# The recurrent state's product: keys scaled for each head on ScalarE, and the copy of px shared

## The chip, the cores and the metric

The kernel runs on one core of one Trainium2 chip, in one launch. The metric is the device time in microseconds (us), the median of several executions. A core has TensorE (PE: matmuls, and the weight loads before them), VectorE (DVE), ScalarE (ACT), GpSimd (POOL) and SyncE (SP, which issues the DMAs here). Each runs its own queue of instructions in order and waits on semaphores for the others.

## The reference

A gated delta-rule attention layer with 32 value heads of width 128 and 16 key heads, followed by a layer norm, a residual, a small gated feed-forward layer, and again layer norm and residual. The input is 4 sequences of 1024 tokens, width 256, in fp32. What concerns the change is the scan over chunks of 64 tokens:

```
def step(St, inp):
    q_i, k_i, u_i, kcd_i, dec_i, g_i = inp
    attn = einsum('bhid,bhjd->bhij', q_i, k_i) * dec_i
    v_new = u_i - einsum('bhid,bhdv->bhiv', kcd_i, St)
    inter = einsum('bhid,bhdv->bhiv', q_i * exp(g_i)[..., None], St)
    out_i = inter + einsum('bhij,bhjv->bhiv', attn, v_new)
    g_last = g_i[..., -1]
    St_new = St * exp(g_last)[..., None, None] + einsum(
        'bhid,bhiv->bhdv', k_i * exp(g_last[..., None] - g_i)[..., None], v_new)
    return (St_new, out_i)
```

The new state is the old one, decayed, plus keys times new values, summed over the 64 tokens of the chunk, where each token has a decay factor of its own for each head. A key head serves two value heads.

## The kernel before

**Tiling.** The 32 heads are taken in 8 groups of 4 (`HG = 4` value heads, `MG = 2` key heads). A tile is 128 rows: a chunk of 64 tokens from each of two sequences, called the halves `ab`. A group has 32 tiles, in four super-blocks of 8. One tile of one group is a step, so there are 256 of them, and the state of two pairs of sequences alternates (`states[p]`). The last two steps of a group need no new state, so 240 steps compute one.

**One step** (`step`, a generator that is resumed in pieces):
- `pv`: values transposed on PE; ACT scales them into `x0` (L675).
- `pkqs` (L684): keys and queries times the state; DVE adds the first into `x0`, four instructions (L695); ACT scales the second into `qs` (L696).
- `px` (L704): `x0` times the inverted matrix, 4 matmuls. `px` is minus the new values, up to a factor for each token. ACT writes `xs`, a negated copy of `px` (L709). Unless the step is a last one, DVE writes `yg`, which is `px` times `ncd` (L712); PE transposes the keys into `pk` (L715), two key heads in one tile each; ACT copies them to `kt` (L717); POOL decays the state (L721).
- `po` (L704): `xs` times the attention matrix; DVE adds `qs` to make `core` (L728). ACT squares `core` (L733).
- `pu` (L741): keys times `yg`, for each key head and each half; the two value heads of a key head stand side by side in 256 columns. DVE adds `pu` to the state (L748).

`ncd` is made for four tiles at a time in `norms` (L502): minus the write strength over the squared norm of the key, times the decay to the end of the chunk.

**What surrounds it.** The program runs as a software pipeline over super-blocks. `channel` makes the convolved projections of later steps: `pp` (L423, wq or wv) on PE, a scaled copy `cv` on ACT (L437), three updates of `cv` on DVE (L440), and a last activation on ACT (L444). `invert` solves the triangular systems on DVE, one rank at a time (L580, L581). `scores` (L530 to L556) and `project_out` (`pz` L143, `zs` L782 to L786, `pto` L790, `oT` L792, `pout` L797, `ac` L802) fill in the rest. The order on every engine is the order of the program, which is written out by hand in a table with a row for each of the eight iterations of a super-block. Two of the rows:

```
SLOTS = [
    ...
    "A v1 O3 N0 v1 T J v1 O4 N1 r Z v1 B N2 q s U",
    ...
    "A v1 O3 N0 v1 T J v1 O4 v1 N1 r Z v1 B N2 q s v1 U",
```

They are rows 1 and 5, counted from 0. `N0`, `N1`, `N2` resume the newest step (`x0`, then `pkqs`, then `px` with `xs`, `yg`, `pk` and `kt`); `O3`, `J`, `O4` resume the one before (`po`, the squares, `pu`); `A` and `B` are `pp` for wv and wq; `v1` is one rank of `invert`; `T`, `Z`, `U` are pieces of `project_out`; `r`, `q`, `s` are `rms`, `roots` and `scores`. In rows 1 and 5 `q` and `s` put activations of other functions on ACT right behind `kt`, with a table load before each kind. "Place n" below means row n of this table, named by the px in it.

**Buffers.** PSUM has a pool of four single banks, taken in turn by `pv`, `pkqs`, `px`, `pk`, `po`, `pz`, `pto`, `pout` and others, and a pool of two double banks, for `pp` and `pu`. A matmul that takes a bank waits until the last reader of its previous tile is through. `xs`, `yg` and `kt` have one buffer each in SBUF.

Of the kernel before, what the change touches and what calls it, by code (L numbers as in the profile page):

```python
# [9 lines left out]
F32 = mybir.dt.float32  # L10
I32 = mybir.dt.int32
AF = mybir.ActivationFunctionType
ALU = mybir.AluOpType

P = 128
# [8 lines left out]
HG = 4  # L24
NG = NV // HG
MG = HG // 2
# [4 lines left out]
SB = 8  # L31
# [28 lines left out]
def bc(ap, shape):  # L60
    return ap.to_broadcast(shape)
# [3 lines left out]
def delta_net_ffn_kernel(  # L65
# [18 lines left out]
    V, A, G_, T_ = nc.vector, nc.scalar, nc.gpsimd, nc.tensor  # L84
# [34 lines left out]
    for ab in range(2):  # L119
        half = slice(ab * C, (ab + 1) * C)  # L120
# [73 lines left out]
    with tc.tile_pool(name="pre", bufs=2) as pre, tc.tile_pool(name="gates", bufs=1) as gp:  # L194
# [38 lines left out]
        u = gp.tile(full, F32, name="u")  # L233
# [75 lines left out]
    with ExitStack() as main:  # L309
        w1 = main.enter_context(tc.tile_pool(name="w1", bufs=1))  # L310
        w2 = main.enter_context(tc.tile_pool(name="w2", bufs=2))
# [4 lines left out]
        def t4(name, bufs=1):  # L316
            return sc.tile([P, HG, P], F32, tag=name, name=name, bufs=bufs)
# [3 lines left out]
        def as4(ps):  # L321
            return ps.rearrange("p (h i) -> p h i", h=HG)
# [128 lines left out]
        def norms(k, blk):  # L451

            if blk == 0:
                k.n2 = w2.tile([P, SB, MG, 2], F32, tag="n2", name="n2", bufs=5)
                k.cc = w2.tile([P, SB, HG], F32, tag="cc", name="cc", bufs=5)
                k.ncd = w2.tile([P, SB, HG], F32, tag="ncd", name="ncd", bufs=5)
                k.ms = w2.tile([P, SB, HG], F32, tag="ms", name="ms", bufs=5)
                k.ltd = sd.tile([P, SB, HG, C], F32, tag="ltd", name="ltd")
                k.atd = sd.tile([P, SB, HG, C], F32, tag="atd", name="atd")
                k.vd, k.vtd = (sd.tile([P, BS, BS], F32, tag=f"vd{i}", name="vd") for i in range(2))  # L460
                k.nd = sd.tile([P, NQ, BS], F32, tag="nd", name="nd")
            us = slice(4 * blk, 4 * blk + 4)

            squares = []
            for m in range(MG):
                for j in range(2):
                    src = k.qk[blk][m][:, :, :, j, :, :].rearrange("p n q a t -> p (n q) (a t)")
                    sq = sc.tile([P, 4, P], F32, tag="sq", name="sq", bufs=4)
                    A.activation(sq, src, AF.Square)
                    squares.append(sq)  # L470
                yield
            ps = bank("pn")
            for q, sq in enumerate(squares):
                T_.matmul(
                    ps[q * BS : (q + 1) * BS, :],
                    lhsT=ones,
                    rhs=sq.rearrange("p i t -> p (i t)"),
                    start=True,
                    stop=True,
                )  # L480
            nT = sc.tile([P, 4, P], F32, tag="sq", name="nT", bufs=4)
            A.copy(nT, as4(ps))
            yield
            ps = bank("pn")
            for i in range(4):
                T_.transpose(as4(ps)[:, i, :], nT[:, i, :], ident)
            n2 = k.n2[:, us]
            V.tensor_scalar_max(
                n2.rearrange("p u m j -> p u (m j)"),
                ps.rearrange("p (u q i) -> p u q i", u=4, i=BS)[:, :, :, 0],  # L490
                NRM2_MIN,
            )
            rk = w2.tile([P, 4, MG], F32, tag="rk", name="rk")
            V.reciprocal(rk, n2[:, :, :, 0])
            t0 = k.t0 + 4 * blk
            V.tensor_tensor(
                k.cc[:, us].rearrange("p u (m h) -> p u m h", h=2),
                dks[k.g][3][:, t0 : t0 + 4, :].rearrange("p u (m h) -> p u m h", h=2),
                bc(rk.unsqueeze(3), [P, 4, MG, 2]),
                ALU.mult,  # L500
            )
            V.scalar_tensor_tensor(  # L502
                k.ncd[:, us], k.cc[:, us], -1.0, dks[k.g][1][:, t0 : t0 + 4, :], ALU.mult, ALU.mult
            )

        def roots(k):
# [151 lines left out]
        def step(k, u):  # L658

            blk, un = divmod(u, 4)  # L660
            n, p = divmod(un, 2)
            ti = k.t0 + u
            ex, _, _, _, el = dks[k.g]
            first = k.first and u < 2
            last = k.last and u >= SB - 2
            S_ = states[p]
            qk, vt = k.qku.pop(u), k.vt[blk]

            pv = bank("pv")
            for h in range(HG):  # L670
                T_.transpose(as4(pv)[:, h, :], vt[h][:, un * P : (un + 1) * P], ident)
            x0 = t4("x0")
            for m in range(MG):
                two = slice(2 * m, 2 * m + 2)
                A.activation(x0[:, two, :], as4(pv)[:, two, :], AF.Copy, scale=k.nnk[:, u, m : m + 1])  # L675
            yield
            if not first:
                got = []
                for j in range(2):
                    ps = bank("pkqs")  # L680
                    for m in range(MG):
                        two = slice(2 * m, 2 * m + 2)
                        for ab in range(2):
                            T_.matmul(  # L684
                                as4(ps)[ab * C : (ab + 1) * C, two, :],
                                lhsT=qk[:, m, j, ab, :],
                                rhs=S_[:, ab, two, :],
                                start=True,
                                stop=True,
                            )  # L690
                    got.append(ps)
                qs = t4("qs")
                for h in range(HG):
                    e = ex[:, ti, h : h + 1]
                    V.scalar_tensor_tensor(x0[:, h, :], as4(got[0])[:, h, :], e, x0[:, h, :], ALU.mult, ALU.add)  # L695
                    A.activation(qs[:, h, :], as4(got[1])[:, h, :], AF.Copy, scale=e)  # L696
            yield

            ue, ae = k.exp.pop(u)

            def applied(w, src, name):
                ps = bank(name)
                for h in range(HG):
                    T_.matmul(as4(ps)[:, h, :], lhsT=w[:, h, :], rhs=src[:, h, :], start=True, stop=True)  # L704
                return ps

            px = applied(ue, x0, "px")
            xs = t4("xs")
            A.activation(xs, as4(px), AF.Copy, scale=-1.0)  # L709
            if not last:  # L710
                yg = t4("yg")
                V.tensor_tensor(yg, as4(px), bc(k.ncd[:, u, :].unsqueeze(2), h4), ALU.mult)  # L712
                pk = bank("pk")
                for m in range(MG):
                    T_.transpose(as4(pk)[:, m, :], qk[:, m, 0].rearrange("p a t -> p (a t)"), ident)  # L715
                kt = sc.tile([P, MG, P], F32, tag="kt", name="kt")
                A.copy(kt, as4(pk)[:, :MG, :])  # L717
                if not first:
                    flat = S_.rearrange("p a h d -> p (a h) d")
                    decay = el[:, ti].rearrange("p a h -> p (a h)").unsqueeze(2)  # L720
                    G_.tensor_tensor(flat, flat, bc(decay, [P, 2 * HG, P]), ALU.mult)  # L721
            yield
            po = applied(ae, xs, "po")
            core = t4("core", OUT_LAG)
            if first:
                V.tensor_copy(core, as4(po))
            else:
                V.tensor_tensor(core, as4(po), qs, ALU.add)  # L728
            k.cores[u] = core
            yield  # L730
            junk = sc.tile([P, P], F32, tag="junk", name="junk")
            for h in range(HG):
                A.activation(junk, core[:, h, :], AF.Square, accum_out=k.ms[:, u, h : h + 1])  # L733
            yield
            if not last:
                pu = two_banks("pu")
                for m in range(MG):
                    two = slice(2 * m, 2 * m + 2)
                    for ab in range(2):
                        half = slice(ab * C, (ab + 1) * C)  # L740
                        T_.matmul(  # L741
                            as4(pu[:, ab])[:, two, :], lhsT=kt[half, m, :], rhs=yg[half, two, :], start=True, stop=True
                        )
                state = S_.rearrange("p a h d -> p (a h d)")
                if first:
                    V.tensor_copy(state, pu.rearrange("p a n -> p (a n)"))
                else:
                    V.tensor_tensor(state, pu.rearrange("p a n -> p (a n)"), state, ALU.add)  # L748
# [410 lines left out]
```

## Time and profile before

| | |
|---|---|
| median of 3 runs | 4344.73 us (4342.15 to 4349.24) |
| profiled execution, its own time | 4347.06 us |
| its span in the trace | 4345.3 us, 79442 instructions |
| mean granted PE clock | 0.98 |
| PE px, 128x128 moving | 2048 records, 287 ns each, 292.9 us busy |
| PE pu, weights 64x128, 64x256 moving | 1920 records, 402 ns each, 272.2 us busy |
| DVE yg, 128x512 | 240, 683 ns each, 164.0 us |
| ACT kt, 128x256 | 240, 374 ns each, 89.6 us |
| ACT xs, 128x512 | 256, 605 ns each, 154.8 us |
| ACT qs, 128x128 with a scale for each partition | 960, 361 ns each, 269.9 us |

How to read it: every fp32 matmul of the program leaves two matmul records and two weight loads in the trace, so the 960 matmuls of `pu` are 1920 records. The records of PE overlap, so the busy time of a group is less than records times mean. In the timelines a row gives the start, the length, the engine, the line, the operation, output and input, and how many instructions were merged; in brackets the idle time before it and what ended that. Rows of the chain of waits give the start, the length, and the engine with its line. A row of the stretches gives PE, PE's weight loads, DVE, ACT and POOL, then the clock and the share of DMA.

### The profile page before, as it was taken

Reading aid. Unit: us, or ns where it says so; the run is one execution under the profiler, and the core shown is the slowest. Engines: PE = TensorE matmul, PEld = TensorE weight load, DVE = VectorE, ACT = ScalarE, POOL = GpSimd, SP = SyncE. Lnnn points to the kernel's source line nnn. Section 1 sums busy time; section 2 is a strip of 40 time slices with the busy share of each in tenths; the row PEclk is TensorE's granted clock in tenths of the full one; section 3 lists DMA queues with packets and bytes.
Section 4 is the critical chain, followed back from the end, with each engine's and each line's share of the span. In section 5 each row is a group of like instructions: output and inputs, shape, how many; then the busy total and the mean of one; then the engine's idle time right before and its main releaser. Section 6 shows DMA issues by size and latency. Waiting matters only on the chain.

```text
span 4345.3 us, 79442 instructions
## 1 busy us (share of the span) xinstructions
PE 3992.3 (92%) x26664; PEld 2858.5 (66%) x26664; DVE 3517.0 (81%) x6641; ACT 2646.9 (61%) x6573; POOL 2082.5 (48%) x1782
## 2 busy tenths in 40 slices
PE   3679999999999999999999999999999999999999
PEld 3456667677666666676766667676766776666454
DVE  4788888888888888888888988888888898886243
ACT  2456667666666666666666666666666666656211
POOL 2545564655555554655455554555554343434122
PEclk7899999999999999999999999999999999999999
DMA  3444444444444454444454444544445444443011
GB/s 88 124 107 113 111 112 124 121 130 119 126 130 118 107 133 125 134 117 119 125 135 128 109 114 128 133 118 114 132 128 128 115 120 121 130 108 96 26 39 29
DMA packets 1053124, 492.72 MB, mean 113 GB/s; under 512 B 730528, under 2 KB 951856, under 8 KB 1052720
## 3 DMA queue, kind: packets, MB, share of 16 engines
q1 hardware_dynamic: 1052720, 487.64, 42.5%
q8 instruction: 216, 3.54, 0.3%
q14 instruction: 188, 1.54, 0.1%
HBM read 267.66 MB, written 219.69 MB: 112 GB/s over the span
## 4 chain that ended last, share of the span: by engine, by line
PE 57%; DVE 25%; issue 7%; ACT 6%; POOL 3%; DMA 1%; SPq 1%; DVEq 0%; POOLq 0%; ACTq 0%
PE pp L423 13%; DVE cv L440 9%; PE pout L797 7%; PE pz L143 7%; PE pkqs L684 6%; DVE rank L580 4%; PE pgu L960 4%; PE px L704 4%; PE pu L741 3%; PE po L704 3%; DVE v L581 2%; PE kkq L546 2%; PE py L976 2%; DVE core L728 2%; PE pto L790 1%
## 5 line engine op out<-in xcount | busy, mean ns | idle before, releaser
L440 DVE SCALAR_TENSOR_TENSOR cv<-pp,cw,cv 128x512 f32<-128x512 f32 x1536 | 1148.9, 748 | 352.2 <-ACT cv L437 322.7
L784 POOL TENSOR_TENSOR zs<-zs,rr 128x512 f32<-128x512 f32 x256 | 267.0, 1043 | 1558.3 <-ACT zs L782 1549.3
L437 ACT ACTIVATE cv<-pp,cw 128x512 f32<-128x512 f32 x512 | 350.9, 685 | 486.0 <-PE pp L423 486.0
L581 DVE TENSOR_TENSOR v<-v,rank 128x31 f32<-128x31 f32 (+15 forms) x992 | 553.3, 558 | 34.1
L423 PE MATMUL pp<-xnT,wq 128*128 128x262 f32 x2048 | 531.0, 401 | 43.3 <-DVE cv L440 34.6
L423 PEld LDWEIGHTS pp<-xnT,wq 128*128 128x128 f32 x2048 | 371.7, 191 | 216.6 <-issue 58.7
L423 PE MATMUL pp<-xnT,wv 128*128 128x262 f32 x2048 | 503.0, 387 | 5.8 <-DVE cv L440 5.8
L797 PE MATMUL pout<-wo,oT 128*128 128x256 f32 x2048 | 504.9, 391 | 0.7 <-ACT oT L792 0.7
L143 PE MATMUL pz<-wzs,xnT 128*64 128x512 f32 x2048 | 487.1, 596 | 4.7 <-DVE ac L802 3.8
L580 DVE TENSOR_TENSOR rank<-v,lb 128x31 f32<-128x31 f32 (+15 forms) x992 | 467.2, 471 | 25.9 <-DMA lb<-ltd 20.1
L684 PE MATMUL pkqs<-S,qku 128*64 128x256 f32 x3840 | 478.1, 387 | 5.2 <-DVE core L728 3.5
L721 POOL TENSOR_TENSOR S<-S,dkm 128x1024 f32<-128x1024 f32 x224 | 436.7, 1949 | 26.5 <-PE pkqs L684 16.1
L704 PE MATMUL px<-x,ue 128*128 128x128 f32 x2048 | 292.9, 287 | 168.2 <-issue 108.1
L704 PEld LDWEIGHTS px<-x,ue 128*128 128x128 f32 x2048 | 264.1, 194 | 269.0 <-issue 151.1
L423 PEld LDWEIGHTS pp<-xnT,wv 128*128 128x128 f32 x2048 | 381.5, 190 | 73.8 <-issue 13.1
L797 PEld LDWEIGHTS pout<-wo,oT 128*128 128x128 f32 x2048 | 384.1, 198 | 49.4 <-issue 3.4
L684 PEld LDWEIGHTS pkqs<-S,qku 128*64 128x64 f32 x3840 | 248.7, 136 | 204.2 <-issue 49.2
L733 ACT ACTIVATE junk<-core 128x128 f32<-128x128 f32 x1024 | 318.5, 311 | 82.4 <-DVE core L728 53.9
L786 POOL TENSOR_TENSOR zs<-zs,core 128x512 f32<-128x512 f32 x256 | 328.6, 1284 | 20.0
L709 ACT ACTIVATE xs<-px 128x512 f32<-128x512 f32 x256 | 154.8, 605 | 236.2 <-PE px L704 236.2
L444 ACT ACTIVATE qk<-cv 128x512 f32<-128x512 f32 x256 | 161.2, 630 | 206.1 <-DVE cv L440 202.6
L741 PE MATMUL pu<-yg,kt 64*128 64x256 f32 x1920 | 272.2, 402 | 14.5 <-DVE cv L440 13.1
(187 smaller groups left out, 7198.4 us busy)
## 6 DMA issues: line engine op xcount, KB each, us to landing
qkd<-qk SPq DMA_DIRECT2D x256, 256.0 KB, 2.6
qku<-qkd SPq DMA_DIRECT2D x256, 256.0 KB, 2.9
dc<-rows_d SPq DMA_DIRECT2D x256, 128.0 KB, 3.4
ltd<-lT SPq DMA_DIRECT2D x128, 256.0 KB, 2.5
atd<-aT SPq DMA_DIRECT2D x128, 256.0 KB, 2.8
ae<-atd SPq DMA_DIRECT2D x512, 64.0 KB, 2.6
acc_d<-ac SPq DMA_DIRECT2D x256, 128.0 KB, 2.2
ac<-acc_d SPq DMA_DIRECT2D x224, 128.0 KB, 2.6
```

Of the source, the lines that this page charges most:

```text
L143: T_.matmul(ps[ab * C : (ab + 1) * C, :], lhsT=xnT[:, kc, 2 * p + ab, H + n * C : H + (n + 1) * C], rhs=rhs(kc), start=kc == 0, stop=kc == ...
L423: T_.matmul(ps[:, 2 * p : 2 * p + 2, : H + BT], lhsT=wt[:, kc, :], rhs=xnT[:, kc, 2 * p : 2 * p + 2, c0 : c0 + H + BT], start=kc == 0, sto ...
L437: A.activation(cv, ps[:, :, H : H + BT], AF.Copy, scale=cw[:, ch, H : H + 1])
L440: V.scalar_tensor_tensor(cv, ps[:, :, i : i + BT], cw[:, ch, i : i + 1], cv, ALU.mult, ALU.add)
L580: V.tensor_tensor(t, bc(v[:, 0 : j + 1, j : j + 1], sh), bc(lb[:, j : j + 1, j + 1 :], sh), ALU.mult)
L581: V.tensor_tensor(v[:, 0 : j + 1, j + 1 :], v[:, 0 : j + 1, j + 1 :], t, ALU.subtract)
L684: T_.matmul(as4(ps)[ab * C : (ab + 1) * C, two, :], lhsT=qk[:, m, j, ab, :], rhs=S_[:, ab, two, :], start=True, stop=True,)
L704: T_.matmul(as4(ps)[:, h, :], lhsT=w[:, h, :], rhs=src[:, h, :], start=True, stop=True)
L721: G_.tensor_tensor(flat, flat, bc(decay, [P, 2 * HG, P]), ALU.mult)
L741: T_.matmul(as4(pu[:, ab])[:, two, :], lhsT=kt[half, m, :], rhs=yg[half, two, :], start=True, stop=True)
L786: G_.tensor_tensor(zs, zs, k.cores.pop(u), ALU.mult)
L797: T_.matmul(pp[:, :HID], lhsT=oT[:, h, :], rhs=wo[:, h, :], start=h == 0, stop=h == HG - 1)
```

## The change

The factor of each token and head moves from the new values to the keys. `norms` makes `cd`, with a positive sign, where it made `ncd`. `yg` is no longer made: `pu` takes `xs`, which `po` takes already. `kt` has one tile for each of the four value heads in place of one for each of the two key heads, and is written by four activations, each with the head's column of `cd` as its scale, from the same two transposed tiles. `pu` becomes eight matmuls with 128 moving columns, in place of four with 256. The scale is per partition since after the transpose the tokens stand in the partitions.

```diff
-                k.ncd = w2.tile([P, SB, HG], F32, tag="ncd", name="ncd", bufs=5)
+                k.cd = w2.tile([P, SB, HG], F32, tag="cd", name="cd", bufs=5)
...
-                k.ncd[:, us], k.cc[:, us], -1.0, dks[k.g][1][:, t0 : t0 + 4, :], ALU.mult, ALU.mult
+                k.cd[:, us], k.cc[:, us], 1.0, dks[k.g][1][:, t0 : t0 + 4, :], ALU.mult, ALU.mult
...
             xs = t4("xs")
             A.activation(xs, as4(px), AF.Copy, scale=-1.0)
             if not last:
-                yg = t4("yg")
-                V.tensor_tensor(yg, as4(px), bc(k.ncd[:, u, :].unsqueeze(2), h4), ALU.mult)
                 pk = bank("pk")
                 for m in range(MG):
                     T_.transpose(as4(pk)[:, m, :], qk[:, m, 0].rearrange("p a t -> p (a t)"), ident)
-                kt = sc.tile([P, MG, P], F32, tag="kt", name="kt")
-                A.copy(kt, as4(pk)[:, :MG, :])
+
+                kt = t4("kt")
+                for h in range(HG):
+                    A.activation(kt[:, h, :], as4(pk)[:, h // 2, :], AF.Copy, scale=k.cd[:, u, h : h + 1])
...
                 pu = two_banks("pu")
-                for m in range(MG):
-                    two = slice(2 * m, 2 * m + 2)
+                for h in range(HG):
                     for ab in range(2):
                         half = slice(ab * C, (ab + 1) * C)
                         T_.matmul(
-                            as4(pu[:, ab])[:, two, :], lhsT=kt[half, m, :], rhs=yg[half, two, :], start=True, stop=True
+                            as4(pu[:, ab])[:, h, :], lhsT=kt[half, h, :], rhs=xs[half, h, :], start=True, stop=True
                         )
```

## The prediction

> **What bounds the kernel now.** I read first the page's busy times and then the stretches of equal length, to see whether one stretch stands for many. Then I read the chain of waits over a quiet stretch, and last the engine timelines of one whole super-block of eight steps.
>
> ```profile
> PE 3992.3 (92%) x26664; PEld 2858.5 (66%) x26664; DVE 3517.0 (81%) x6641; ACT 2646.9 (61%) x6573; POOL 2082.5 (48%) x1782
> ...
> 2000.00:2500.00 500.00, 475.74 (x3321) 348.06 (x3319) 434.00 (x798) 336.60 (x847) 256.67 (x220) 0.99 0.47 126
> ...
> 2004.28 0.87 PE kkq L546 x16
> 2007.12 0.89 PE px L704 x8
> 2008.23 1.73 PE pout L797 x8
> 2013.49 1.06 PE pu L741 x8
> ```
>
> TensorE (PE) is busy for 475.7 of 500 us in the middle, VectorE (DVE) for 434.0, ScalarE (ACT) for 336.6. PE is the bound, and a step (240 full ones, about 15 us each) can get shorter only where PE stands still. The chain rows price PE's bursts: 16 half-width kkq matmuls in 0.87 us, 8 px matmuls in 0.89, 8 pu in 1.06.
>
> Laying each px against the start of the matmul before it shows where PE stands still: behind px's operand x0, and nearly only at three of the eight places of a super-block. In order of place (rows 5, 6 and 7 of the slot table) the sums are about 62, 44 and 53 us. Typical stalls are 2.8, 2.2 and 1.6 us, in 22, 22 and 29 super-blocks. The places before them look like this:
>
> ```profile
> 2039.39 0.68 DVE L712 TENSOR_TENSOR yg<-px,ncd 128x512 f32<-128x512 f32 x1
> 2039.99 0.90 DVE L580 TENSOR_TENSOR rank<-v,lb 128x112 f32<-128x112 f32 x1
> ...
> 2053.28 1.11 DVE L695 SCALAR_TENSOR_TENSOR x<-pkqs,dkm,x 128x128 f32<-128x128 f32 x4
> ...
> 2053.72 1.22 PE L704 MATMUL px<-x,ue 128*128 128x128 f32 x8 [2.63 <-issue]
> ```
>
> DVE works from yg to the four x0 updates without a pause, and px starts 0.44 us after the first of them. The row says "issue", but what is late is DVE's queue. The next place has ACT's queue beside it:
>
> ```profile
> 2055.47 0.37 ACT L717 COPY kt<-pk 128x256 f32<-128x256 f32 x1
> 2055.85 1.28 ACT L765 ACT_TABLE_LOAD   x1
> ...
> 2061.67 0.67 ACT L437 ACTIVATE cv<-pp,cw 128x512 f32<-128x512 f32 x1
> 2062.24 0.83 ACT L675 ACTIVATE x<-pv,nnk 128x256 f32<-128x256 f32 x2
> ...
> 2065.58 1.12 ACT L696 ACTIVATE qs<-pkqs,dkm 128x128 f32<-128x128 f32 x4
> ...
> 2062.61 2.31 DVE L440 SCALAR_TENSOR_TENSOR cv<-pp,cw,cv 128x512 f32<-128x512 f32 x3
> ```
>
> After kt, ACT works without a pause through three table loads to cv, which ends at 2062.34. DVE takes that cv up at 2062.61. So here ACT is only 0.27 us ahead of the engine that decides the next stall.
>
> **The change part by part.**
>
> *DVE, yg removed.* 240 instructions of 683 ns; the next one starts 0.60 us later (2039.39 to 2039.99), so 0.60 us a step leaves DVE's queue. It is worth something only where DVE runs without a pause up to a late x0. At places 5 and 7 I find no other wait in that run: at place 7 the core addition starts 7.1 us after px, while po is there after 5.8, so 0.60 less is still not too early. That gives 22 x 0.60 = 13.2 us at place 5 and 29 x 0.60 = 17.4 us at place 7. At the other places PE itself is late and the time becomes DVE idleness. Bounds for one place: nothing (a cv from ACT ends last) and 0.68 (the whole instruction).
>
> *ACT, kt in four scaled copies of 128x128.* Before, the copy held the queue for 0.38 us (2055.47 to 2055.85). The nearest row is qs, the same form (PSUM, a scale per partition, 128x128): four in 1.12 us. So ACT is 0.75 us later behind every kt. At six of eight places ACT then has 0.9 to 2.9 us of idleness before the next instruction that anyone needs, or within one or two short instructions, and this covers it. If that cover were gone, each would behave like places 5 and 1, which follow.
> The kt of place 5, with three table loads behind it, decides the stall at place 6: 0.75 less the 0.27 us of lead, and 0.03 for the hand-over, puts DVE's cv 0.51 later, with yg gone or not, and x0 and px with it. In 15 super-blocks the lead is about 0.27, in 7 it is 0.03 to 0.1 (DVE already waits for ACT there, up to 1.0 us), which makes some 0.70: 15 x 0.51 + 7 x 0.70 = 12.6 us lost. This takes back what place 5 wins.
> At place 1 (the other one with table loads) the square root's input holds ACT for 0.33 us already, so 0.42 of the 0.75 arrive. There pz waits for the PSUM bank that the copy x<-pv (L675) reads. Its end at 2002.29 and pz's start at 2002.35 stand together in 28 super-blocks: 28 x 0.42 = 11.8 us lost, which no later place gives back, since PE is the bound up to place 4.
>
> *PE, pu in 8 matmuls of 128 columns in place of 4 of 256.* In records (two passes each) 16 and not 8, and 16 weight loads. Now 1.06 us is four pairs (the two 64-row halves run together) at pout's pitch for 256 columns, 1.73/8 = 0.216, which is 0.86, and 0.20 before the first pair. Then it is eight pairs. By px (128 columns, a new weight tile of 128 columns each time, 0.89/8 = 0.111) that is 0.89 + 0.20; by kkq (pairs, 0.87/8 = 0.109) 0.87 + 0.20. I take 0.02 us a step: 240 x 0.02 = 5 us lost. No row has pairs of 64x128 weights with 128 columns, so the bounds are wide: +0.01 a step (2 us) where both halves load together, and, where the sixteen stand one behind the other at px's pitch, 16 x 0.111 - 0.86 = +0.92 a step, 220 us. No gain is possible, since the column count is the same. I take the low end. In pu's first two pairs today the weight loads start 0.109 us apart, pair to pair, which is the time of one load in px.
>
> *Waits that go.* In the first super-block of seven groups PE waits at places 5 and 6 for pto, pu and pp, 27 us together, with DVE behind all of them (pto partly for yg's reading of the px bank). DVE is 0.60 earlier at each of the two: 7 x 1.2 = 8 us won.
>
> *Nothing for the rest.* cd in place of ncd is the same instruction. pu now waits for xs and kt on ACT, which are done some 6 us before pu's turn at place 4 (2039.38 against 2044.4) and 1 to 2 us earlier than yg was. The built order of every engine keeps its places, and the DMAs are the same ones.
>
> *The clock.* Fifteen times in the loop the granted clock falls to one half for 3.4 us, each time behind a 2.8 us stall (the eight pout rows then take 3.4 us, not 1.7). The 2.8 at place 5 becomes 2.2, the 2.2 at place 6 becomes 2.7. I count it as moved, not as won or lost.
>
> *The sum:* -13.2 + 12.6 - 17.4 + 11.8 + 5 - 8 = -9 us against the profiled execution's own 4347.06 (its span is 4345.3), 4338. That execution lies 2.3 above the median of the runs, 4344.73. So 4335.5, and I write 4335.
>
> **Two rules of the Trainium skill that speak against it.** The TensorE page (TensorE: Matmul & The Clock Gate, Part 3, The mechanism) says that a weight load overlaps a running matmul only when the row groups differ. The px rows disagree: their loads fill all rows and still come at the pitch of the matmuls alone, 0.111 us. By the rule, each pair's loads would wait for its predecessor of the same rows, an estimate of 0.86 us more a step or some 205 us, and the kernel would be near 4540. ScalarE: Activation LUTs (What ACT_TABLE_LOAD costs) gives 186 ns + 0.833 ns an element + 93 ns for a pointer scale, 386 ns for one scaled copy, with 93 ns of overlap between neighbours. The qs row has 361 and a pitch of 250 ns. By the page the four would take 1.27 us, an estimate, so 0.14 more than I use, and behind places 1 and 5 together 7 us more.
>
> **The rivals.**
> *The gain is whole.* If ACT's later cv is covered behind places 1 and 5 after all (its lead is larger once DVE stalls less, or the scaled copies run closer), the three stalls all give 0.60: 22 + 22 + 29 = 73 times, 44 us, 8 more in the first super-blocks, less 5 for pu: 4298. For it: DVE is idle before none of these x0. Against: the 0.27 us of lead.
> *The clock decides, slower.* If the wait at place 6 passes the length at which the half clock comes and place 5's still does at times, 22 super-blocks pay 1.7 us there, 37 us, against some 11 saved (15 events, of which 0.9 of 1.7 us is now swallowed by the following stall): -9 + 26 = +17, 4362. It decides from the point where place 6's stall reaches the 2.8 us behind which all events now stand. Against: by the sum it reaches 2.75 in 15 and 2.5 in 7.
> *The weight loads decide, slower.* As bounded above: from 9 ns more per pair in pu on (240 x 8 x 0.009 = 18 us, the 9 won and 9 of noise) the kernel is measurably slower than before, and with no pairing at all it is 4335 + 220 - 5 = 4550. Against: px's pitch.
> That the change does not do what it says, I exclude: the built order shows yg gone, kt as four activations and pu as eight matmuls.
>
> **How the numbers follow.** Forecast case 0.50, its own range 4320 to 4350; whole gain 0.18; clock 0.20; weight loads 0.12. What a measurement can tell from no change is 0.2%, 8.7 us: faster is below 4336, slower above 4353. The forecast lies on that edge: 0.26 faster, 0.20 same, 0.04 slower. The whole gain is faster (0.18). The clock case gives 0.05 same and 0.15 slower, the weight loads 0.01 and 0.11. Together 0.44, 0.26, 0.30. The range takes in the whole gain and most of the clock case: 4292 to 4372. It leaves the far part of the weight loads out.
>
> **What would show it.** In the profile of the changed kernel: DVE's busy time down by 164 us, ACT's up by some 250; pu bursts of about 1.08 us in the chain; px's stalls about 2.2, 2.7 and 1.0 at the three places; DVE waiting for ACT's cv at place 6; pz starting with the end of L675 at place 1, 0.4 us later after px. I am wrong if pu takes 1.3 us or more, if place 6's stall shrinks too, or if half-clock stretches are many more than fifteen.

## The result, and the profile after

| | before | after |
|---|---|---|
| median | 4344.59 us (4 runs, 4342.15 to 4349.24) | 4372.86 us (4 runs, 4370.38 to 4378.11) |
| ratio | | 1.0065, 95% interval 1.0048 to 1.0083 |
| span of the profiled execution | 4345.3 us | 4372.4 us |
| mean granted PE clock | 0.98 | 0.975 |

The changed kernel is slower by 0.65%, some 28 us. That is 38 us above the forecast and just outside the range. The page of the changed kernel gives the busy times, and its stretch in the middle (PE, weight loads, DVE, ACT, POOL, clock, share of DMA, GB/s) answers to the one shown of before:

```profile
PE 4008.7 (92%) x28584; PEld 2936.7 (67%) x28584; DVE 3377.2 (77%) x6401; ACT 2831.6 (65%) x7293; POOL 2076.7 (47%) x1782
...
2000.00:2500.00 500.00, 474.12 (x3544) 356.78 (x3537) 414.54 (x769) 355.57 (x927) 261.82 (x223) 0.99 0.46 121
```

PE is the bound as before, but it stands still a little more (busy 474.1 of 500 us, before 475.7). ACT took 185 us on. DVE's busy time fell by 140 us. The 240 instructions that are gone were 164.0 us long, but the busy time counts overlapping instructions once, and the next instruction started 0.60 us behind the start of yg: 240 x 0.60 = 144 us could go. Over the whole kernel, then, nearly all of it went; what counts is where. Three groups of the page:

```profile
L143 PE MATMUL pz<-wzs,xnT 128*64 128x512 f32 x2048 | 497.2, 607 | 39.3 <-ACT x L675 32.0
...
L704 PE MATMUL px<-x,ue 128*128 128x128 f32 x2048 | 292.0, 286 | 168.6 <-issue 124.9
...
L740 PE MATMUL pu<-xs,kt 64*128 64x128 f32 x3840 | 278.9, 285 | 11.6 <-DVE cv L440 9.7
```

PE now waits 32 us for ACT's copy out of the pv bank (L675) before pz. The px group waits longest, as before. pu's 3840 half-width records cost 278.9 us, against 272.2 for 1920 full-width ones.

Where the time went, in sums over the loop (the fourth px to the last) from one px to the next, in us (the row of place 5, say, runs from its px to that of place 6, so it holds place 6's stall):

| from the px of place | before | after | difference |
|---|---|---|---|
| 0 | 426.2 | 427.6 | +1.4 |
| 1 | 449.3 | 467.3 | +18.0 |
| 2 and 3 | 946.5 | 947.3 | +0.8 |
| 4 (holds the stall at 5) | 459.3 | 457.9 | -1.4 |
| 5 (holds the stall at 6) | 507.2 | 526.1 | +18.9 |
| 6 (holds the stall at 7) | 492.0 | 480.7 | -11.3 |
| 7 | 444.3 | 443.1 | -1.2 |

The losses stand where they were forecast, at places 1 and 5, larger than forecast. The gain at place 4's step is missing. The DVE and POOL timelines of the changed kernel there show why:

```profile
1814.65 2.32 DVE L440 SCALAR_TENSOR_TENSOR cv<-pp,cw,cv 128x512 f32<-128x512 f32 x3 [2.25 <-ACT cv L437]
1816.89 1.48 DVE L580 TENSOR_TENSOR rank<-v,lb 128x112 f32<-128x112 f32 x1
1818.41 1.00 DVE L581 TENSOR_TENSOR v<-v,rank 128x112 f32<-128x112 f32 x1
...
1828.38 1.13 DVE L580 TENSOR_TENSOR rank<-v,lb 128x192 f32<-128x192 f32 x1
1829.54 1.31 DVE L581 TENSOR_TENSOR v<-v,rank 128x192 f32<-128x192 f32 x1
1830.77 1.11 DVE L695 SCALAR_TENSOR_TENSOR x<-pkqs,dkm,x 128x128 f32<-128x128 f32 x4
```

```profile
1816.33 1.91 POOL L721 TENSOR_TENSOR S<-S,dkm 128x1024 f32<-128x1024 f32 x1
1818.19 1.09 POOL L530 TENSOR_TENSOR dc<-dc,dkm 128x512 f32<-128x512 f32 x1
...
1828.25 1.04 POOL L783 TENSOR_TENSOR zs<-zs,rr 128x512 f32<-128x512 f32 x1 [2.71 <-ACT zs L781]
1829.37 1.26 POOL L785 TENSOR_TENSOR zs<-zs,core 128x512 f32<-128x512 f32 x1
```

The rank instruction took 0.90 us before, behind yg, and ended at 2040.89, just behind the end of the same decay of the state on POOL at 2040.76:

```profile
2038.86 1.90 POOL L721 TENSOR_TENSOR S<-S,dkm 128x1024 f32<-128x1024 f32 x1
```

Now it starts in yg's place and takes 1.48, on the same 112 elements. Its end, 1818.37, is again just behind the end of the decay, at 1818.24. From yg's start to x0's start it was 13.89 us before (2039.39 to 2053.28); from this rank's start to x0's it is 13.88. The 0.60 us are gone without a trace in x0. It is so in all 22 super-blocks that have this stall: this rank takes 0.90 to 1.01 us before and 1.47 or 1.48 after. In place 4's step as a whole, the time of rank instructions above their shortest form goes from 113.0 to 124.7 us. At x0 itself each half of the pair ends some 0.2 us behind a POOL instruction (1829.29 and 1829.51, then 1830.63 and 1830.85), and x0 starts 0.14 us behind the end of POOL's product of zs with core. PE shows that px, and the stall before it, are as they were:

```profile
1831.21 1.22 PE L704 MATMUL px<-x,ue 128*128 128x128 f32 x8 [2.63 <-issue]
```

### The profile page after: what moved, and what is told of

It reads as the page before. It is cut to its first block, busy times and chain, and to the rows that moved or that the text cites. A ratio compares the mean times of both kernels' runs of the same rounds, so it can differ in the third digit from the quotient of the medians.

```text
span 4372.4 us, 83748 instructions
## 1 busy us (share of the span) xinstructions
PE 4008.7 (92%) x28584; PEld 2936.7 (67%) x28584; DVE 3377.2 (77%) x6401; ACT 2831.6 (65%) x7293; POOL 2076.7 (47%) x1782
## 4 chain that ended last, share of the span: by engine, by line
PE 72%; ACT 12%; DVE 9%; issue 4%; DMA 1%; POOL 1%; SPq 1%; ACTq 0%; POOLq 0%; DVEq 0%
PE pp L423 17%; PE pz L143 9%; PE pout L796 8%; PE pkqs L684 8%; PE px L704 6%; PE pu L740 4%; PE pgu L959 4%; PE po L704 4%; DVE cv L440 3%; PE kkq L546 2%; ACT cv L437 2%; PE py L975 2%; PE pto L789 2%; PE pv L671 2%; DVE rank L580 2%
## 5 line engine op out<-in xcount | busy, mean ns | idle before, releaser
L440 DVE SCALAR_TENSOR_TENSOR cv<-pp,cw,cv 128x512 f32<-128x512 f32 x1536 | 1150.1, 749 | 465.3 <-ACT cv L437 429.9
L581 DVE TENSOR_TENSOR v<-v,rank 128x31 f32<-128x31 f32 (+15 forms) x992 | 523.6, 528 | 34.1
L143 PE MATMUL pz<-wzs,xnT 128*64 128x512 f32 x2048 | 497.2, 607 | 39.3 <-ACT x L675 32.0
L580 DVE TENSOR_TENSOR rank<-v,lb 128x31 f32<-128x31 f32 (+15 forms) x992 | 480.0, 484 | 26.6 <-DMA lb<-ltd 20.5
L684 PE MATMUL pkqs<-S,qku 128*64 128x256 f32 x3840 | 468.1, 386 | 0.0
L721 POOL TENSOR_TENSOR S<-S,dkm 128x1024 f32<-128x1024 f32 x224 | 437.0, 1951 | 28.2 <-PE pkqs L684 11.3
L785 POOL TENSOR_TENSOR zs<-zs,core 128x512 f32<-128x512 f32 x256 | 328.4, 1283 | 20.0
L143 PEld LDWEIGHTS pz<-wzs,xnT 128*64 128x64 f32 x2048 | 142.9, 138 | 241.3 <-issue 152.0
L740 PE MATMUL pu<-xs,kt 64*128 64x128 f32 x3840 | 278.9, 285 | 11.6 <-DVE cv L440 9.7
```

The lines of the kernel that those rows point to most:

```text
L143: T_.matmul(ps[ab * C : (ab + 1) * C, :], lhsT=xnT[:, kc, 2 * p + ab, H + n * C : H + (n + 1) * C], rhs=rhs(kc), start=kc == 0, stop=kc == ...
L440: V.scalar_tensor_tensor(cv, ps[:, :, i : i + BT], cw[:, ch, i : i + 1], cv, ALU.mult, ALU.add)
L580: V.tensor_tensor(t, bc(v[:, 0 : j + 1, j : j + 1], sh), bc(lb[:, j : j + 1, j + 1 :], sh), ALU.mult)
L581: V.tensor_tensor(v[:, 0 : j + 1, j + 1 :], v[:, 0 : j + 1, j + 1 :], t, ALU.subtract)
L684: T_.matmul(as4(ps)[ab * C : (ab + 1) * C, two, :], lhsT=qk[:, m, j, ab, :], rhs=S_[:, ab, two, :], start=True, stop=True,)
L740: T_.matmul(as4(pu[:, ab])[:, h, :], lhsT=kt[half, h, :], rhs=xs[half, h, :], start=True, stop=True)
```

## The experiments

Two readings are told apart in what follows. In A, DVE's queue is made of instructions of fixed lengths, and x0 is late because of what stands before it; this is the prediction's reading. In B, an instruction of the rank pair (L580 and L581, both of whose inputs are in SBUF) that meets a POOL instruction lasts until that one is through, so POOL sets when x0 starts. Such an instruction is called held, and its held time is what it lasts above the shortest one of the same line and size in any of the runs. The medians of before beside these runs were 4345.69, 4345.15, 4346.71 and 4345.25 us.

**ACT's part alone.** yg stays, kt is written by four scaled copies with a scale of one.

```diff
-                kt = sc.tile([P, MG, P], F32, tag="kt", name="kt")
-                A.copy(kt, as4(pk)[:, :MG, :])
+                kt = t4("kt")
+                for h in range(HG):
+                    A.activation(kt[:, h, :], as4(pk)[:, h // 2, :], AF.Copy, scale=ones[:, 0:1])
...
-                            as4(pu[:, ab])[:, two, :], lhsT=kt[half, m, :], rhs=yg[half, two, :], start=True, stop=True
+                            as4(pu[:, ab])[:, two, :], lhsT=kt[half, 2 * m, :], rhs=yg[half, two, :], start=True, stop=True
```

> The kernel before, with kt written by four scaled copies of 128x128 on ScalarE (the scale is a column of ones) and all else kept: yg stays, pu stays in four matmuls. Theory A (the one on record: VectorE's own queue decides the stalls in front of px; ScalarE's 0.75 us arrive at places 1 and 5 only): place 1 loses 28 x 0.42 to 0.75, place 5 loses 22 x 0.51 to 0.70 and there is nothing to win, so 25 to 35 us slower, about 4372. Theory B (GpSimd, started by ScalarE's zs, holds VectorE's pair of rank updates ahead of x0): zs is later by the whole 0.75 where ScalarE has no idle time, so place 5's step is 0.75 longer; 28 x 0.6 + 22 x 0.75 = 33 us, about 4378. It tells what the ScalarE part costs; A and B part by under 10 us here.

Measured: 4386.24 us, ratio 1.0096 (1.0082 to 1.0110), +41. Place 1's step is 18.6 longer, place 5's 13.6. So ACT's 0.75 us a step costs far more than the forecast's 24.4, and more than either reading expected (some 27 and 33).

**DVE's part alone.** No yg; pu takes xs, and kt is one copy with a constant scale. The decay factors of token and head are left out.

```diff
-                yg = t4("yg")
-                V.tensor_tensor(yg, as4(px), bc(k.ncd[:, u, :].unsqueeze(2), h4), ALU.mult)
...
-                A.copy(kt, as4(pk)[:, :MG, :])
+                A.activation(kt, as4(pk)[:, :MG, :], AF.Copy, scale=0.02)
...
-                            as4(pu[:, ab])[:, two, :], lhsT=kt[half, m, :], rhs=yg[half, two, :], start=True, stop=True
+                            as4(pu[:, ab])[:, two, :], lhsT=kt[half, m, :], rhs=xs[half, two, :], start=True, stop=True
```

> The kernel before without yg: pu takes xs, kt stays one copy of 128x256 (times 0.02 in place of the factors for each token and head, which are left out, so that the state stays finite). Only VectorE's 683 ns a step go. Theory A: all three stalls in front of px shrink by 0.60, 73 x 0.60 = 44 us, and some 8 in the first super-blocks: about 4293. Theory B: x0 starts when GpSimd's zs is through, whatever VectorE's queue holds, so the stall at place 5 stays at 2.8, and the kernel is 0 to 15 us faster: 4330 to 4345.

Measured: 4329.88 us, ratio 0.9968 (0.9956 to 0.9980), -15.8 where the prediction had -38.6. That is the fast end of B's range; A had 4293. Its page:

```profile
PE 3990.0 (92%) x26664; PEld 2862.9 (66%) x26664; DVE 3433.9 (79%) x6401; ACT 2652.4 (61%) x6573; POOL 2075.5 (48%) x1782
```

240 x 0.60 = 144 us could go from DVE's busy time, and it falls from 3517.0 to 3433.9, by 83. Over all rank instructions the held time is 367 us before and 418 here: 51 of the 61 us that come back are holds. Place 5's stall keeps its 2.8 us.

**PE's part alone.** pu in eight matmuls of 128 columns, all else as before.

```diff
-                for m in range(MG):
-                    two = slice(2 * m, 2 * m + 2)
+                for h in range(HG):
...
-                            as4(pu[:, ab])[:, two, :], lhsT=kt[half, m, :], rhs=yg[half, two, :], start=True, stop=True
+                            as4(pu[:, ab])[:, h, :], lhsT=kt[half, h // 2, :], rhs=yg[half, h, :], start=True, stop=True
```

> The kernel before with pu in eight matmuls of 128 columns (each key tile loaded twice), yg and kt kept. A and B alike: 240 x 0.02 = 5 us slower at most, 4345 to 4351, and a pu burst of about 1.08 us in the chain. If the weight loads of 64x128 tiles did not run as pairs, +0.9 us a step: 4560.

Measured: 4348.69 us, ratio 1.0007 (0.9998 to 1.0016), +3. The weight loads are no rival any more. The three parts alone sum to 41 - 15.8 + 3 = +28, which is what the whole change does.

**POOL's multiplication out.** Before, without the multiplication of zs by rr (L784): the normalisation of the result rows is left out.

```diff
-            G_.tensor_tensor(zs, zs, bc(k.rr[u // 4][:, u % 4, :].unsqueeze(2), h4), ALU.mult)
```

> The kernel before without GpSimd's multiplication of zs by rr (1.04 us a step; the normalisation of the output rows is left out). Nothing on VectorE changes. Theory A: VectorE's queue is as long as before, so the stalls in front of px stay and the time is within 10 us of before. Theory B: GpSimd is through with zs 1.1 us earlier, so at places 5, 6 and 7 x0 and px come up to 1.1 us earlier: 73 x 0.8 to 1.1, 58 to 80 us faster, 4265 to 4290.

Measured: 4371.89 us, ratio 1.0066 (1.0054 to 1.0079): slower, with an instruction less. Neither reading gave this number. The DVE and POOL timelines ahead of place 5's x0 show what happened:

```profile
1829.21 1.35 DVE L580 TENSOR_TENSOR rank<-v,lb 128x192 f32<-128x192 f32 x1
1830.60 1.93 DVE L581 TENSOR_TENSOR v<-v,rank 128x192 f32<-128x192 f32 x1
1832.45 1.11 DVE L695 SCALAR_TENSOR_TENSOR x<-pkqs,dkm,x 128x128 f32<-128x128 f32 x4
```

```profile
1829.08 1.26 POOL L785 TENSOR_TENSOR zs<-zs,core 128x512 f32<-128x512 f32 x1 [3.35 <-ACT zs L782]
1830.30 2.01 POOL L721 TENSOR_TENSOR S<-S,dkm 128x1024 f32<-128x1024 f32 x1
```

With the 1.04 us multiplication gone, the pair's second half no longer meets the 1.26 us product of zs with core but the 2.0 us decay behind it, and lasts 1.93 us in place of 1.31. The stall goes from 2.79 to 3.23 us here. PE's idle time in front of px goes from 59.6, 41.1 and 52.8 us in sum at places 5, 6 and 7 to 67.0, 49.2 and 61.9: 24.6 us more, of the 26. By A no DVE instruction should have changed.

**The decay out as well.** The decisive run: POOL's decay of the state (L721) is left out too.

```diff
-                if not first:
-                    flat = S_.rearrange("p a h d -> p (a h) d")
-                    decay = el[:, ti].rearrange("p a h -> p (a h)").unsqueeze(2)
-                    G_.tensor_tensor(flat, flat, bc(decay, [P, 2 * HG, P]), ALU.mult)
...
-            G_.tensor_tensor(zs, zs, bc(k.rr[u // 4][:, u % 4, :].unsqueeze(2), h4), ALU.mult)
```

> The kernel before without two of POOL's instructions: the multiplication of zs by rr (so the normalisation of a result row is left out) and the decay of S (so the state isn't decayed). What is left on POOL beside the rank pair at places 5 to 7 is the addition into zs alone, 1.26 us. Theory B (an instruction of the rank pair that meets a POOL instruction lasts until that one is through): the pair's first half is held by the addition, the second is free (some 0.35 us instead of 1.31), so x0 comes about 1 us earlier at places 5, 6 and 7; place 5's stall of px falls from 2.79 to 1.5 to 1.9 us, and with three places in some 22 blocks the kernel is 40 to 80 us faster, 4265 to 4305. Theory A (DVE's own queue, instructions of fixed lengths): no DVE instruction changes, the stalls stay within 0.1 us and the time within 10 us of 4345, or at the 4372 of the run that left only the multiplication out, if something else of that edit costs it.

Measured: 4217.24 us, ratio 0.9706 (0.9693 to 0.9719), -128 us. Nothing was taken out of DVE, yet its page has 254 us less of DVE work than before (3517.0):

```profile
PE 3960.5 (94%) x26664; PEld 2852.7 (68%) x26664; DVE 3263.1 (77%) x6641; ACT 2643.8 (63%) x6573; POOL 1384.7 (33%) x1302
```

POOL's one instruction left there is the product of zs with core (the expectation calls it an addition). The same pair ahead of place 5's x0, first before, with POOL beside it, then here:

```profile
2050.89 1.13 DVE L580 TENSOR_TENSOR rank<-v,lb 128x192 f32<-128x192 f32 x1
2052.05 1.31 DVE L581 TENSOR_TENSOR v<-v,rank 128x192 f32<-128x192 f32 x1
```

```profile
2050.76 1.04 POOL L784 TENSOR_TENSOR zs<-zs,rr 128x512 f32<-128x512 f32 x1 [3.19 <-ACT zs L782]
2051.88 1.26 POOL L786 TENSOR_TENSOR zs<-zs,core 128x512 f32<-128x512 f32 x1
```

```profile
1997.66 0.35 DVE L580 TENSOR_TENSOR rank<-v,lb 128x192 f32<-128x192 f32 x1
1998.05 0.36 DVE L581 TENSOR_TENSOR v<-v,rank 128x192 f32<-128x192 f32 x1
1998.32 1.12 DVE L695 SCALAR_TENSOR_TENSOR x<-pkqs,dkm,x 128x128 f32<-128x128 f32 x4
```

```profile
1998.56 1.27 POOL L781 TENSOR_TENSOR zs<-zs,core 128x512 f32<-128x512 f32 x1 [5.12 <-ACT zs L778]
```

1.13 becomes 0.35 and 1.31 becomes 0.36, since the pair is through before POOL starts. These are its lengths in all 22 super-blocks, and their stalls at place 5, 61.4 us in sum, are gone. A reader set free by the missing instructions is no rival: in the trace of before no other engine's wait is put down to the decay, and PE's waits for zs, 10 us at most, all lie behind 4008 us. A is out, and B had the sign and the mechanism. Its size was 1.6 to 3 times too small: it took one half of the pair for held and counted x0 some 1 us earlier, where both are free and x0 stands 5.35 us behind its cv in place of 7.08, so 1.73 earlier. By the two groups of the pages, rank instructions account for 195 of the 254 us (1020.5 to 825.3); small DVE products such as the one that makes ncd account for part of the rest (a median of 936 ns before, 175 here).

Not every POOL instruction holds the pair. In the trace of before, 440 rank instructions began inside a TENSOR_TENSOR of POOL (two tiles in) that would have outlasted them by over 60 ns, and all 440 were longer than their shortest form, by 0.25 us or more. Another 154 began inside POOL's TENSOR_SCALAR (L301, one tile in). Not one of these lasted to its end, and 114 kept their own length to within 60 ns.

**The pair behind x0.** If POOL holds the pair, x0 can go ahead of it. In rows 4 to 7 of the slot table the rank between O4 and N1 moves behind N1 (row 5 as an example):

```diff
-            "A v1 O3 N0 v1 T J v1 O4 v1 N1 r Z v1 B N2 q s v1 U",
+            "A v1 O3 N0 v1 T J v1 O4 N1 v1 r Z v1 B N2 q s v1 U",
```

This was run on before, on the changed kernel, and on the mixed kernel that comes last.

> The kernel before with one order changed on VectorE: in rows 4 to 7 of the slot table the rank pair that stands between S and x0 comes behind x0. Theory A (a queue of fixed lengths): x0 is earlier by the pair's own free length, 0.85 us, once in each run of VectorE without a pause: 22 x 0.85 = 19 us faster, 4326. Theory B (each of the pair's two instructions lasts until the GpSimd instruction that it meets is through, 2.3 to 2.5 us together): x0 is earlier by 2.4 us at place 5, and since VectorE works without a pause from place 4 to 7 the later stalls keep what is left: 22 x 2.4 = 53 us faster or more, 4285 to 4295.

> The changed kernel with x0 ahead of the rank pair (the order of the run with x0 first). That run lost its place 5 stall (53 us) but paid 150 us at pto, waiting for yg, and at pu, waiting for cv. Theory B: with yg gone and px free as soon as xs is through, the pto waits (74 us) go, and some of pu's; ScalarE's 41 us stay: 4384.75 - 74 - 20 + 41 = 4332, between 4300 and 4350. Theory A: removing yg is worth the 16 us that it was worth alone: 4384.75 - 16 + 41 = 4410.

> The hybrid (kt on VectorE in steps 0 and 4 alone, ScalarE else) with x0 ahead of the rank pair. Theory B: as the changed kernel with x0 first, without ScalarE's loss at the table places, so 42 us below that one, about 4290 (4260 to 4320), and faster than both kernels. Theory A: the sum of the two single runs, 4330 + 40 = 4370.

Measured: on before 4384.75 us, 1.0087 (1.0072 to 1.0103); on the changed kernel 4375.98, 1.0067 (1.0054 to 1.0079), no gain over its own 1.0065; on the mixed kernel 4356.23, 1.0022 (1.0013 to 1.0031), a loss of 26 us. On before, place 4's step did shrink from 459.3 to 405.8 us, but the steps of 6 and 7 grew by 20 and 62. PE's waits on before, and then on the changed kernel (us, times, longest):

```profile
PE pto L790 <- DVE yg L712: 74.1, 79, 1.5
PE pu L741 <- DVE cv L440: 73.9, 113, 2.3
```

```profile
PE pu L740 <- DVE cv L440: 103.1, 79, 2.0
...
PE pz L143 <- ACT x L675: 24.4, 28, 1.0
```

The wait did not go, it moved to other readers of DVE. The pair meets POOL further on: the held time is 399, 416 and 408 us in the three, more than the 367 before. All three miss the numbers of both readings, B's ranges by 90, 26 and 36 us and A's by 59, 34 and 14. B tells how long the pair lasts, but the estimates made with it left out the readers that wait next.

**Both pairs behind px.** In the same rows the last two ranks before N2 move behind it:

```diff
-            "A v1 O3 N0 v1 T J v1 O4 v1 N1 r Z v1 B N2 q s v1 U",
+            "A v1 O3 N0 v1 T J v1 O4 N1 r Z B N2 q s v1 v1 v1 U",
```

> The kernel before with both rank pairs of rows 4 to 7 that stand between S and px moved behind px, out of the stretch in which GpSimd does zs, zs and the state's decay. Theory A: as in the run with x0 first, 4326, since the same work is only later. Theory B: the pairs are held far less, 1.5 us a place less VectorE time as well, so the three stalls mostly go: 80 to 140 us faster, 4205 to 4265.

> The hybrid with both rank pairs of rows 4 to 7 behind px. Theory B: that order paid 74 us at pto, waiting for yg, at place 4; these go, and the hybrid's 15: 4361 - 74 - 15 = 4272 (4250 to 4310). Theory A: 4361 - 15 = 4346.

Measured: on before 4361.35 us, 1.0033 (1.0021 to 1.0046); on the mixed kernel 4350.36, 1.0006 (0.9997 to 1.0015). Both are slower than all that B expected; A's 4346 is near for the second, not for the first. The held time falls to 325 and 346 us, and on before the steps of 5 and 6 get 12 and 37 us shorter, but place 4's gets 42 longer, where pto now waits 69 us for DVE. An order that gains at every place was not found. DVE, holds included, is nearly full there: in before it stands idle for 53 of the 1443 us of the steps of places 5, 6 and 7.

**The product of the keys on DVE.** The changed kernel, with one DVE product of 128x512 in place of ACT's four copies; then the same only in the two steps of a super-block whose kt has table loads behind it (places 5 and 1, `u` 0 and 4), and ACT's copies in the others.

```diff
-                for h in range(HG):
-                    A.activation(kt[:, h, :], as4(pk)[:, h // 2, :], AF.Copy, scale=k.cd[:, u, h : h + 1])
+                V.tensor_tensor(
+                    kt.rearrange("p (m h) i -> p m h i", h=2),
+                    bc(as4(pk)[:, :MG, :].unsqueeze(2), [P, MG, 2, P]),
+                    bc(k.cd[:, u, :].rearrange("p (m h) -> p m h", h=2).unsqueeze(3), [P, MG, 2, P]),
+                    ALU.mult,
+                )
```

> The changed kernel with kt written by one VectorE product of 128x512 (pk times cd for each head) in place of ScalarE's four copies. VectorE carries the same load as before the change, ScalarE 0.38 us a step less than before it. If ScalarE's queue at places 1 and 5 is the cause of the loss (A and B agree on this): 28 x 0.38 + 22 x 0.38 = 19 us won against before, 3 lost for pu: about 4330. If the loss lies in pu or in the sharing of xs, it stays near 4370.

> The changed kernel with kt on VectorE (one product) in steps 0 and 4 of a super-block, whose kt stands in front of the table loads (places 5 and 1), and on ScalarE (four copies) in the other six. ScalarE alone as the cause: both table places now win 0.38 each instead of losing 0.45 to 0.77, 19 us, and the other places lose nothing: 4345 - 19 + 3, about 4328, and a few us less where VectorE is freed (the run without yg showed 16 us for all eight places). If it is as slow as the change, places other than 1 and 5 pay.

Measured: 4328.95 us, 0.9961 (0.9948 to 0.9973), and 4330.01, 0.9964 (0.9951 to 0.9976). Both beat both kernels, by some 16 and 44 us, and can't be told apart. With the product on DVE everywhere, DVE works nearly as long as before (3505.7 us for 3517.0) and ACT 62 us less: place 1's step falls from 449.3 to 441.4, below before. So the changed kernel's loss is ACT's, and at the two places with table loads.

## Why the prediction was wrong

| term, us | forecast | in the changed kernel |
|---|---|---|
| place 5, yg gone | -13.2 | 0.0 (PE idle before px 61.4, then 61.4) |
| place 7, yg gone | -17.4 | -13.7 (52.8, then 39.1) |
| first super-blocks | -8 | -13 (26.7, then 13.8) |
| place 6, kt of place 5 | +12.6 | +13.8 (42.5, then 56.3) |
| place 1, pz | +11.8 | +18.0 |
| place 5, pz behind L675 | none | +10.4, in 17 super-blocks |
| pu | +5 | +3 (alone) |
| sum | -9 | +18.5 |

PE's idle times are the starts of bursts laid against the usual pitch of the same two bursts. The measured span grew by 27. The 9 us that the terms leave stand beside eight more stretches of half clock, and were not separated further. Of the 36 us between the forecast's -9 and the 27, then, 13.2 are place 5's, 10.4 a wait of pz that was put at nothing, 6.2 place 1's size, and 9 open; the other terms nearly cancel.

**The step that failed** is the one on DVE: "It is worth something only where DVE runs without a pause up to a late x0. At places 5 and 7 I find no other wait in that run". There was one, and the timeline shows no gap for it: it is inside the instructions. A rank of 192 elements was read as 1.13 us of work, where 0.35 is its own and the rest POOL's. It was in the trace of before: the 175-element rank just ahead of that one took 0.34 us.

```profile
2049.12 0.34 DVE L580 TENSOR_TENSOR rank<-v,lb 128x175 f32<-128x175 f32 x1
```

Lengths that differ by a factor of three for nearly the same size were not asked about. At place 5 the 0.60 us vanish whole, in the ranks behind the missing yg. At place 7, yg's removal alone brings 5.1 us and not 17.4, largely for the same reason: in most super-blocks the first rank of the pair there (240 elements) takes 0.97 to 1.11 us where it took 0.83, and some 0.3 us reach x0. That the table has 13.7, near the forecast, is luck. In 17 super-blocks the stall is some 0.3 us shorter; in five it is gone. There the half clock behind place 6's stall delays PE (po is through 7.42 us after px, in the others 5.74), POOL's products start later by as much, and the pair runs free (0.40 and 0.41 us). With ACT's part alone, place 7 gets 6.5 back too.

The Trainium skill states the rule that was missed (SBUF — State Buffer, Who interferes with whom): a VectorE instruction with two SBUF inputs contends with a GpSimd instruction that reads SBUF, and the one that is second is blocked, not slowed. The runs agree for POOL's TENSOR_TENSORs: 1.13 against 0.35 us for the same instruction. For POOL's TENSOR_SCALAR, which reads SBUF too, they do not: none of 154 rank instructions was held to its end. cv (L440), whose only full-size input in SBUF is cv itself, keeps its mean of 748 ns with POOL busy 2082 us or 1385.

**ACT, place 5's kt.** Right in mechanism and size: +13.8 for +12.6. DVE's cv waits for ACT's, and place 6's stall is 2.71 us (forecast 2.7). The ACT and DVE rows of the changed kernel:

```profile
1832.95 1.14 ACT L717 ACTIVATE kt<-pk,cd 128x128 f32<-128x128 f32 x4
1834.11 1.28 ACT L764 ACT_TABLE_LOAD   x1
...
1839.93 0.67 ACT L437 ACTIVATE cv<-pp,cw 128x512 f32<-128x512 f32 x1
```

```profile
1840.63 2.32 DVE L440 SCALAR_TENSOR_TENSOR cv<-pp,cw,cv 128x512 f32<-128x512 f32 x3 [2.18 <-ACT cv L437]
```

The four copies take 1.14 us, as the qs row said (1.12), and not 1.27. But the same delay also reached pz at place 5 through L675 in 17 super-blocks (10.4 us), a reader of the late ACT queue that the forecast followed at place 1 only.

**ACT, place 1.** The mechanism was right, the size 6 us low. The forecast took 0.33 us off everywhere for a wait that ACT had already. The steps of before are 14.53 us long in 13 super-blocks, where this holds, and 14.21 in 15, where nothing covers the 0.75. After, 28 are 14.98 or more: 13 x 0.45 + 15 x 0.77 = 17.4. The last link, ACT and PE in the changed kernel:

```profile
2023.78 0.83 ACT L675 ACTIVATE x<-pv,nnk 128x256 f32<-128x256 f32 x2
```

```profile
2024.67 1.94 PE L143 MATMUL pz<-wzs,xnT 128*64 128x512 f32 x8 [0.87 <-ACT x L675]
```

**PE.** Right: +3 alone for +5, and bursts of 1.09 us for 1.08. The 205 us of the rule that spoke against it did not come.

**The clock.** "Moved, not as won or lost" was wrong. Half-clock stretches in the loop went from 16 (58.0 us; the prediction counts fifteen) to 24 (81.9 us). Not all of before stood behind a 2.8 us stall: ten stood at place 5's, and four at place 7's in a group's first super-block, which is some 2.4 us. After, place 5's stall kept its length and seven of its ten stretches, and five begin at place 6's stall of 2.71 us, where none did. Six begin at place 5 in a first super-block, behind a wait of pu of up to 1.4 us and one of pz (for DVE's addition ac, L801) that grew from 0.63 to 1.04 us. The rival in which the clock decides had this in it and named a near time, 4362; but it supposed place 5's stall to shrink, and it priced nothing of pz. Its price of 1.7 us a stretch does not hold at place 6 either: in the changed kernel that step lasts 15.66 us with the half clock and 15.24 without, since place 7's stall is gone.

**The signs named.** DVE was to fall by 164 us: 140. ACT was to rise by some 250: 185. In both the busy time counts overlapping instructions once (240 x 0.60 = 144 and 240 x 0.75 = 180). Stalls of 2.2, 2.7 and 1.0 us were named: 2.8, 2.7 and 1.3.

## What to carry to other kernels

Before an instruction is taken out of a full queue, compare the lengths of one operation at like sizes. Where they differ by a factor of three, as here, ask which other engine's instruction each long one ends with; what is saved ahead of it may be waited out in it. Delay put on an engine with table loads behind it has to be followed to every reader of that queue, and the cover has to be counted super-block by super-block, not on the one that is looked at. A product can be moved to the engine with room place by place: here the keys' product on DVE is worth 16 us over before, where on ACT it costs 28.

## What the runs showed of the hardware

- POOL and DVE: the same rank of 192 elements takes 0.35 us alone and 1.13 to 1.35 us beside POOL, and a product of 128x16 elements 0.17 against 0.97 us. In the kernel before, the rank instructions hold 367 us of such time, over a third of their 1020.5. It is POOL's TENSOR_TENSORs that hold them (440 of 440 by 0.25 us or more), not its TENSOR_SCALAR (none of 154 to its end). POOL pays hardly anything: its product of zs with core takes 1283 ns in the changed kernel and 1274 in the run without the multiplication by rr and the decay.
- Taking one POOL instruction out made the kernel 0.66% slower, and taking two out made it 2.9% faster. In the first the pair at place 5 met a longer instruction, in the second none. Whether that work can be kept and done off POOL with the same gain was not tried.
